# Ten row tiles of a Strassen-style projection are turned by VectorE blocks instead of TensorE transposes

## The chip, the cores and the metric

The kernel runs on one core of a Trainium2 chip. The core has TensorE (PE in the profile; its weight loads are the row PEld), VectorE (DVE), ScalarE (ACT), GpSimd (POOL) and SyncE (SP), which here only issues DMAs. The engines run side by side, each through its own queue in order. The metric is the device time of one execution in microseconds, as a median over runs.

## The reference

One graph attention layer over 2708 nodes of 1024 features, in float32, with a sparse 0/1 adjacency (about four neighbours a row):

```python
h = jnp.maximum(_layernorm(x, axis=-1), 0.0)
q = h @ W_q.T + b_q
k = h @ W_k.T + b_k
v = h @ W_v.T + b_v
z = scale * (q @ k.T)
spare_z = z * adj
spare_z = jnp.where(spare_z == 0.0, -10000.0, spare_z)
attn = jax.nn.softmax(spare_z, axis=1)
x = x + jax.nn.relu(attn @ v)
```

## The kernel before

**The mathematics.** W_q and W_k are folded into one matrix M, so that the score of an edge is the dot product of a row of `q = h M + b` with the neighbour's row of h. W_v is applied after the weighted sum: `u` is the sum of the neighbours' h rows by their softmax weights, and the output is `x + relu(u W_v + b)`. Nodes are sorted by their number of neighbours and cut into 21 full tiles of 128 rows; tile t has K[t] neighbour slots, from 1 to 15.

**Two products of tiles.** Both `h M` and `u W_v` are worked in pairs of row tiles (`units`: ten pairs of kind `q`, then ten of kind `o`, then one tile alone). A pair is a Strassen-style product with seven block products instead of eight (`multiply`, `opened`, `add_block`). Each of the seven is eight matmuls of 128x512 on PE as the chain shows them, four calls in the program, each in two passes. Its left operands are blocks of the turned (transposed) pair: `a11` and `a12`, the halves of the first tile, `a22`, a half of the second, and `s1 = a22 + a21`, `s3 = a11 - a21`, `s2 = s1 - a11`, `s4 = a12 - s2`. The right operands lie in `M` and `T` in SBUF. In a pair PE goes through `s2`, `a12`, `s4`, `s3`, then the first two products of the next pair (`a11`, `s1`), then `a22`.

**Where the operands come from.** `blocks` (L677) makes them one pair ahead, in two steps: `upper` (L692) at place 0 of the pair before, `lower` (L696) at place 2; the places are the calls of `after(i)` between the products. `half_turned` (L397) has PE transpose four 128x128 blocks into a PSUM bank; ScalarE copies the bank for `a11`, `a12` and `a22` (L684), VectorE adds and subtracts `a21` straight from PSUM for `s1` and `s3` and makes `s2` and `s4` (L688). Only in two early pairs are `s2` and `s4` on GpSimd.

**The stream.** Between those, VectorE works through the attention (`scores`, `weights`, `sums`): a multiply with a running sum for each neighbour slot (L826, output `junk`), small steps for the softmax, and a multiply-add for each slot (L879, into `u`). GpSimd gathers the neighbour rows by indirect DMA into 13 slots (`fill`, L805, and `gather`, L594); a slot is gathered anew as soon as it is read out. `advance(share)` at each place lets the stream go on by a quota of nominal microseconds, 19 for a pair of kind `o`. The order of VectorE's instructions is the program's (a manual schedule); ScalarE, GpSimd and SyncE are ordered by the framework's scheduler in this stretch.

**The tiles through DRAM.** The stream runs ahead of the `o` pairs. A finished `u` that is needed soon stays in SBUF (`near`, L933, `held`). Ten of the 21, tiles 6, 5, 4, 3, 2, 0, 1 and 20, 18, 19, are written to `u_dram` (L888) and read back into `or` tiles by one DMA each (L1142). The pairs are (6,5), (4,3), (2,0), (1,7), (13,12), (11,10), (14,9), (15,16), (20,17), (18,19), and tile 8 alone. Row tiles come from one ring of seven buffers (`row_tile`).

**The PSUM banks.** Each pair has banks X, Z and Y. Y starts as a copy of X that ScalarE makes (L961, `psy<-ps`) once `a11` is in X; the product with `s2` is added to this copy, so PE's first product of a pair needs it. ScalarE's queue also holds steps of the stream, which wait for VectorE.

## Time and profile before

| what | value |
|---|---|
| time of the runs | median 647.43 us (647.41 to 647.71, 3 runs) |
| profiled execution, its span | 641.9 us |
| TensorE busy | 635.2 us (99%) |
| VectorE busy | 521.9 us (81%) |
| GpSimd, ScalarE busy | 377.3 us (59%), 279.6 us (44%) |
| stretch of one `o` pair | 25.8 us |
| DMA | mean 294 GB/s |

The pairs of kind `o` start at about 372 us, and from 346 us on their operands are made. Each row of a timeline below gives the start in microseconds from the span's beginning, the duration, the engine, the line, the operation, the tiles out<-in with their shapes, and in brackets the idle time before it and what ended it. A row with x2 at its end is two instructions merged. In a row of waits the numbers are the total in microseconds, the number of waits and the longest.

### The profile page before, as it was taken

Reading aid. Unit: us, or ns where it says so; the run is one execution under the profiler, and the core shown is the slowest. Engines: PE = TensorE matmul, PEld = TensorE weight load, DVE = VectorE, ACT = ScalarE, POOL = GpSimd, SP = SyncE. Lnnn points to the kernel's source line nnn. Section 1 sums busy time; section 2 is a strip of 40 time slices with the busy share of each in tenths; the row PEclk is TensorE's granted clock in tenths of the full one; section 3 lists DMA queues with packets and bytes.
Section 4 is the critical chain, followed back from the end, with each engine's and each line's share of the span. In section 5 each row is a group of like instructions: output and inputs, shape, how many; then the busy total and the mean of one; then the engine's idle time right before and its main releaser. Section 6 shows DMA issues by size and latency. Waiting matters only on the chain.

```text
span 641.9 us, 6381 instructions
## 1 busy us (share of the span) xinstructions
PE 635.2 (99%) x1731; PEld 326.2 (51%) x1731; DVE 521.9 (81%) x1014; ACT 279.6 (44%) x426; POOL 377.3 (59%) x400
## 2 busy tenths in 40 slices
PE   9999999999999999999999999999999999999996
PEld 5777766444544444444444454454454444444442
DVE  5999788997895755998888959997999989989121
ACT  3539974849775622423223132433342344333300
POOL 2649960875858457755735525665685856872431
PEclk9999999999999999999999999999999999999999
DMA  8999997598798969998977998988898989995542
GB/s 338 407 366 314 345 346 295 189 358 301 264 358 317 363 201 404 355 359 257 322 260 275 419 416 267 327 272 255 240 328 272 283 331 304 281 285 125 146 139 95
DMA packets 61986, 189.02 MB, mean 294 GB/s; under 512 B 10701, under 2 KB 11037, under 8 KB 61048
## 3 DMA queue, kind: packets, MB, share of 16 engines
q0 software_dynamic: 27888, 84.95, 41.6%
q1 hardware_dynamic: 29994, 89.36, 37.7%
q10 hardware_dynamic: 4062, 14.24, 5.9%
q8 instruction: 16, 0.26, 0.2%
q14 instruction: 26, 0.21, 0.1%
HBM read 159.81 MB, written 42.31 MB: 315 GB/s over the span
## 4 chain that ended last, share of the span: by engine, by line
PE 98%; DMA 1%; DVE 0%; POOL 0%; POOLq 0%; issue 0%
PE ps L948 45%; PE psy L948 32%; PE ps_y L463 6%; PE pt L402 6%; PE ps_x L463 4%; PE ps_z L463 4%; DMA wlow<-in_wq_dram 1%; PE ps_h L1153 0%; PE ps_v L581 0%; DVE y_alone L1297 0%; POOL out_dram L1281 0%; POOLq L1303 0%; PE ps_all L664 0%; PE ps_in L662 0%; PE ps_b L728 0%
## 5 line engine op out<-in xcount | busy, mean ns | idle before, releaser
L597 POOL DMA_INDIRECT g<-h_dram,tab x105 | 124.8, 1188 | 70.4 <-ACT u L871 19.1
L948 PE MATMUL ps<-M,a 128*128 128x512 f32 x320 | 144.0, 593 | 0.0
L948 PE MATMUL psy<-wlow,s 128*128 128x512 f32 x320 | 143.9, 592 | 0.0
L826 DVE SCALAR_TENSOR_TENSOR junk<-g,pq 128x1024 uint8<-128x1024 f32 x93 | 114.0, 1226 | 9.8 <-DMA g<-h_dram,tab 7.3
L879 DVE SCALAR_TENSOR_TENSOR u<-g,coef,u 128x1024 f32<-128x1024 f32 x79 | 101.4, 1283 | 5.6 <-ACT u L871 3.7
L948 PEld LDWEIGHTS ps<-M,a 128*128 128x128 f32 x320 | 59.3, 190 | 68.0 <-issue 67.4
L948 PEld LDWEIGHTS psy<-wlow,s 128*128 128x128 f32 x320 | 59.2, 190 | 66.8 <-issue 65.8
L376 DVE FIND_INDEX8 at<-ones,adj 128x8 uint32<-128x685 f32 (+1 forms) x88 | 74.5, 865 | 0.0
L948 PE MATMUL psy<-wlow,a 128*128 128x512 f32 x160 | 71.9, 592 | 0.0
L948 PE MATMUL ps<-M,s 128*128 128x512 f32 x160 | 71.9, 592 | 0.0
L948 PE MATMUL ps<-wlow,s 128*128 128x512 f32 x160 | 71.9, 592 | 0.0
L355 ACT ACTIVATE sized<-adj 128x2708 uint8<-128x2708 f32 (+1 forms) x22 | 54.3, 2468 | 7.7 <-DMA adj<-in_adj_dram 6.4
L285 POOL TENSOR_TENSOR hsum<-hsum,x 128x256 f32<-128x256 f32 (+1 forms) x56 | 38.6, 726 | 26.3 <-DVE wlow L431 22.3
L1047 POOL DMA_INDIRECT y<-in_x_dram,tab x19 | 33.5, 1763 | 30.8 <-ACT taken L1013 11.2
L948 PEld LDWEIGHTS psy<-wlow,a 128*128 128x128 f32 x160 | 30.4, 190 | 38.3 <-issue 37.8
L948 PEld LDWEIGHTS ps<-wlow,s 128*128 128x128 f32 x160 | 30.4, 190 | 38.3 <-issue 37.6
L948 PEld LDWEIGHTS ps<-M,s 128*128 128x128 f32 x160 | 30.3, 190 | 38.1 <-issue 37.4
L778 POOL DMA_INDIRECT out_dram<-y,tab x21 | 28.4, 1353 | 19.3 <-DMA y<-in_x_dram,tab 11.6
L684 ACT COPY a<-pt 128x512 f32<-128x512 f32 x60 | 33.4, 590 | 3.1 <-PE pt L402 3.1
L597 POOL DMA_INDIRECT M<-h_dram,tab x20 | 24.2, 1212 | 13.4 <-ACT u L871 4.7
L688 DVE TENSOR_TENSOR s<-a,pt 128x512 f32<-128x512 f32 x40 | 25.6, 681 | 7.8 <-ACT a L684 7.8
L871 ACT ACTIVATE u<-g,coef 128x1024 f32<-128x1024 f32 x16 | 18.4, 1149 | 27.1 <-DVE coef L870 26.3
(238 smaller groups left out, 847.9 us busy)
## 6 DMA issues: line engine op xcount, KB each, us to landing
adj<-in_adj_dram SPq DMA_DIRECT2D x21, 1354.0 KB, 12.0
x<-in_x_dram SPq DMA_DIRECT2D x21, 512.0 KB, 8.0
h_dram<-x ACTq DMA_DIRECT2D x21, 512.0 KB, 7.2
q_late<-q SPq DMA_DIRECT2D x12, 512.0 KB, 6.9
pq<-q_late SPq DMA_DIRECT2D x12, 512.0 KB, 4.8
u_dram<-u SPq DMA_DIRECT2D x10, 512.0 KB, 6.5
or<-u_dram SPq DMA_DIRECT2D x10, 512.0 KB, 8.2
g<-in_wv_dram SPq DMA_DIRECT2D x16, 256.0 KB, 8.3
```

Of the source, the lines that this page charges most:

```text
L285: small.append(nc.gpsimd.tensor_add(hsum[:n, cols], hsum[:n, cols], xt[:n, cols]))
L355: nc.scalar.activation(sized[:n], a[:n, :, :PW], AF.Abs, accum_out=total[:n, t:t + 1])
L376: nc.vector.max_index(at[:n, k - first_k, g, :], ones[:n, 0:8], a[:n, g, :])
L402: nc.tensor.transpose(pt[:, c, :], xt[:, k * P:(k + 1) * P], ident)
L463: mm = nc.tensor.matmul(bank, a_tile(o + H * a[0], a[1], i), b(o), start=first and o == 0, stop=(o == H - 1), skip_group_check=True)
L597: return nc.gpsimd.indirect_dma_start(out=dst, out_offset=None, in_=src, in_offset=off, bounds_check=N - 1, oob_is_err=False)
L684: nc.scalar.copy(ops[name], bank)
L778: to = nc.gpsimd.indirect_dma_start(out=out, out_offset=bass.IndirectOffsetOnAxis(ap=ptab.bitcast(U32)[:n, t, SLOTS:SLOTS + 1], axis=0), i ...
L826: chained(lambda: nc.vector.scalar_tensor_tensor(junk, g_of[t][s], 1.0, tq[t], op0=ALU.mult, op1=ALU.mult, accum_out=zall[:, t, s:s + 1]))
L879: chained(lambda: nc.vector.scalar_tensor_tensor(u, g_of[t][s], coef[:, at[t][s]:at[t][s] + 1], u, op0=ALU.mult, op1=ALU.add))
L948: mm = nc.tensor.matmul(bank, a[:, c, :], b[:, c, :], start=False, stop=(c == 3), skip_group_check=True)
L1047: return nc.gpsimd.indirect_dma_start(out=y[:n], out_offset=None, in_=x, in_offset=off, compute_op=ALU.add)
```

## The change

The ten tiles that go through DRAM are no longer transposed by TensorE. VectorE can transpose 32-by-32 blocks inside each group of 32 partitions; what must move between the groups of partitions is moved by the DMA.

- When `u` of such a tile is done, ScalarE copies it once into a tile `v` in which the columns stand in quarter order (columns (c, a, r) at (a, c, r), with a one of four quarters and r one of 32), and `v` is written to `u_dram`.
- The tile is read back by four DMAs (`by_quarters`). Quarter a of the columns of all 128 rows lands on 32 partitions, in pieces of 256 elements (1 KB).
- `faces` is one VectorE instruction that transposes 128 partitions x 512 elements in 32-by-32 blocks and writes the half in its final order, straight into the operand tile in SBUF. `upper` makes `a11` and `a12` by it, `lower` `a22` and, in the tile of `s3`, `a21`; `s1` and `s3` are then made of SBUF operands.
- In a pair with such a tile (six pairs) `s2` and `s4` go to GpSimd.
- The stream's quota is cut by 0.75 nominal microseconds for each such tile of the next pair.

```diff
+QUADS = 4
+QP = P // QUADS
+FACED = (6, 5, 4, 3, 2, 0, 1, 20, 18, 19)
...
+    faced = []
+
+    def by_quarters(dst, rows):
+
+        faced.append(dst)
+        for a in range(QUADS):
+            cols = slice(a * D // QUADS, (a + 1) * D // QUADS)
+            nc.sync.dma_start(dst[a * QP:(a + 1) * QP, :].rearrange("r (g j) -> r g j", g=QUADS),
+                              rows[:, cols].rearrange("(g r) j -> r g j", r=QP))
+
+    def faces(dst, xt, lo, hi):
+
+        return nc.vector.transpose(dst.rearrange("p c (g r) -> p g c r", r=QP),
+                                   xt.rearrange("p (g c r) -> p g c r", g=QUADS, r=QP)[:, :, lo:hi])
+
+    def is_faced(xt):
+        return any(xt is y for y in faced)
+
...
+        def faced_half(name, xt, s):
+            ops[name] = small(name).rearrange("p (c q) -> p c q", q=P)
+            faces(ops[name], xt, s * 4, s * 4 + 4)
+
         def upper():
-            held("a11", half_turned(xa, 0))
-            held("a12", half_turned(xa, 1))
+            for s, name in enumerate(("a11", "a12")):
+                if is_faced(xa):
+                    faced_half(name, xa, s)
+                else:
+                    held(name, half_turned(xa, s))
 
         def lower():
-            held("a22", half_turned(xb, 1))
-            a21 = half_turned(xb, 0)
-            put("s1", ops["a22"], a21, ALU.add)
-            put("s3", ops["a11"], a21, ALU.subtract)
+            if is_faced(xb):
+                faced_half("a22", xb, 1)
+                faced_half("s3", xb, 0)
+                put("s1", ops["a22"], ops["s3"], ALU.add)
+                behind.append(nc.vector.tensor_sub(ops["s3"], ops["a11"], ops["s3"]))
+            else:
+                held("a22", half_turned(xb, 1))
+                a21 = half_turned(xb, 0)
+                put("s1", ops["a22"], a21, ALU.add)
+                put("s3", ops["a11"], a21, ALU.subtract)
             put("s2", ops["s1"], ops["a11"], ALU.subtract, eng)
             put("s4", ops["a12"], ops["s2"], ALU.subtract, eng)
...
-        if near(t):
+        if t in FACED:
+            v = row_tile(f"v_{t}")
+            nc.scalar.copy(v.rearrange("p (a c r) -> p c a r", a=QUADS, r=QP),
+                           u.rearrange("p (c a r) -> p c a r", a=QUADS, r=QP))
+            nc.sync.dma_start(u_dram[t * P:(t + 1) * P, :], v)
+        elif near(t):
             held[t] = u
...
-                nc.sync.dma_start(rows[-1], u_dram[t * P:(t + 1) * P, :])
+                if t in FACED:
+                    by_quarters(rows[-1], u_dram[t * P:(t + 1) * P, :])
+                else:
+                    nc.sync.dma_start(rows[-1], u_dram[t * P:(t + 1) * P, :])
...
         nxt = units[n + 1] if n + 1 < len(units) else None
+        if nxt is not None and nxt[0] == "o":
+            share -= 0.75 / 7 * len(set(nxt[1:]) & set(FACED))
...
-                    ops_of[n + 1] = blocks(*rows_of[n + 1], nc.gpsimd if n + 1 < FIRST - 1 else None)
+                    ops_of[n + 1] = blocks(*rows_of[n + 1], nc.gpsimd if n + 1 < FIRST - 1 or any(
+                        is_faced(xt) for xt in rows_of[n + 1]) else None)
```

How the instructions stand. On VectorE, the operands of the pair (6,5) amid the sums of tile 0, before (the sums s1 to s4 are all named s with a number, in the order s1, s3, s2, s4; `pt` is the bank that PE transposed into):

```order
L879 SCALAR_TENSOR_TENSOR u_2300<-g_1404,coef,u_2300 128x1024
L688 TENSOR_TENSOR s_2369<-a_2362,pt 128x512
L688 TENSOR_TENSOR s_2371<-a_2324,pt 128x512
L688 TENSOR_TENSOR s_2373<-s_2369,a_2324 128x512
L688 TENSOR_TENSOR s_2375<-a_2331,s_2373 128x512
L879 SCALAR_TENSOR_TENSOR u_2300<-g_1405,coef,u_2300 128x1024
```

and in the change (a_2335 and a_2337 are the halves of tile 6, a_2363 and s_2365 those of tile 5):

```order
L913 SCALAR_TENSOR_TENSOR u_2316<-g_1400,coef,u_2316 128x1024
L692 STREAM_TRANSPOSE a_2335<-or_2254 128x4x4x32
L692 STREAM_TRANSPOSE a_2337<-or_2254 128x4x4x32
L913 SCALAR_TENSOR_TENSOR u_2316<-g_1401,coef,u_2316 128x1024
L913 SCALAR_TENSOR_TENSOR u_2316<-g_1402,coef,u_2316 128x1024
L913 SCALAR_TENSOR_TENSOR u_2316<-g_1403,coef,u_2316 128x1024
L913 SCALAR_TENSOR_TENSOR u_2316<-g_1404,coef,u_2316 128x1024
L692 STREAM_TRANSPOSE a_2363<-or_2259 128x4x4x32
L692 STREAM_TRANSPOSE s_2365<-or_2259 128x4x4x32
L709 TENSOR_TENSOR s_2367<-a_2363,s_2365 128x512
L729 TENSOR_TENSOR s_2365<-a_2335,s_2365 128x512
L913 SCALAR_TENSOR_TENSOR u_2316<-g_1405,coef,u_2316 128x1024
```

Four block transposes have come in, and s2 and s4 have gone. They stand on GpSimd now, between two gathers of that pair's time:

```order
L600 DMA g_1403<-h_dram,tab 128x1024
L600 DMA g_1404<-h_dram,tab 128x1024
L709 TENSOR_TENSOR s_2370<-s_2367,a_2335 128x512
L709 TENSOR_TENSOR s_2372<-a_2337,s_2370 128x512
L600 DMA g_1405<-h_dram,tab 128x1024
```

where before the gathers stood behind each other. On ScalarE, around the copy `psy<-ps` that starts bank Y of the pair (14,9), before (w and m belong to tile 20 of the stream):

```order
L1013 COPY taken<-psy 128x512
L860 ACTIVATE w_3285,m_3324<-w_3285,m_3324 128x2
L865 ACTIVATE u_3326<-hsum,m_3324 128x1024
L1064 ACTIVATE y_3249<-u_3292 128x512
L961 COPY psy<-ps_3338 128x512
```

and in the change:

```order
L1052 COPY taken<-psy 128x512
L1103 ACTIVATE y_3217<-u_3259 128x512
L894 ACTIVATE w_3253,m_3304<-w_3253,m_3304 128x2
L1000 COPY psy<-ps_3292 128x512
L1003 COPY p_3359<-ps_3294 128x512
L899 ACTIVATE u_3306<-hsum,m_3304 128x1024
```

The 1024-element activation of tile 20 has moved behind the copy; the exponential, which waits for VectorE, still stands ahead of it. On VectorE, the operands of the last pair (18,19) amid the sums of tile 8, before:

```order
L879 SCALAR_TENSOR_TENSOR u_3675<-g_1400,coef,u_3675 128x1024
L688 TENSOR_TENSOR s_3776<-a_3769,pt 128x512
L688 TENSOR_TENSOR s_3778<-a_3745,pt 128x512
L688 TENSOR_TENSOR s_3780<-s_3776,a_3745 128x512
L688 TENSOR_TENSOR s_3782<-a_3752,s_3780 128x512
L879 SCALAR_TENSOR_TENSOR u_3675<-g_1401,coef,u_3675 128x1024
```

and in the change:

```order
L913 SCALAR_TENSOR_TENSOR u_3642<-g_1399,coef,u_3642 128x1024
L692 STREAM_TRANSPOSE a_3726<-or_3672 128x4x4x32
L692 STREAM_TRANSPOSE s_3728<-or_3672 128x4x4x32
L709 TENSOR_TENSOR s_3730<-a_3726,s_3728 128x512
L729 TENSOR_TENSOR s_3728<-a_3712,s_3728 128x512
L913 SCALAR_TENSOR_TENSOR u_3642<-g_1400,coef,u_3642 128x1024
L913 SCALAR_TENSOR_TENSOR u_3642<-g_1401,coef,u_3642 128x1024
```

One multiply-add of tile 8 more stands behind the pair's s1.

## The prediction

> **What bounds the kernel now.** I read the page's engine shares and its chain of waits first, then the chain in order of time, then VectorE (DVE), GpSimd (POOL) and ScalarE (ACT) in the timeline around the ten tiles.
>
> ```profile
> span 641.9 us, 6381 instructions
> PE 635.2 (99%) x1731; PEld 326.2 (51%) x1731; DVE 521.9 (81%) x1014; ACT 279.6 (44%) x426; POOL 377.3 (59%) x400
> PE 98%; DMA 1%; DVE 0%; POOL 0%; POOLq 0%; issue 0%
> ```
>
> TensorE (PE) is the chain: 98% of the span. The profiled execution's span is 641.9 us, the median of the runs 647.43, so 5.5 us lie around the span; I make the sum on the span and add the difference to 647.43. Where DVE and POOL stand while the `o` pairs are worked, one pair's stretch to a row:
>
> ```profile
> core 0: us, PE busy (x) PEld busy (x) DVE busy (x) ACT busy (x) POOL busy (x), PEclk, DMA share, GB/s
> 346.86:372.65 25.79, 25.79 (x75) 12.30 (x73) 23.67 (x27) 5.46 (x10) 14.90 (x13) 1.00 1.02 411
> 475.79:501.57 25.78, 25.78 (x74) 12.29 (x73) 25.25 (x41) 9.14 (x17) 16.89 (x15) 1.00 0.91 302
> 578.93:604.71 25.78, 25.78 (x74) 12.29 (x73) 16.75 (x29) 7.32 (x13) 8.19 (x6) 1.00 0.51 132
> ```
>
> PE never pauses, but DVE is busy 23.67 and 25.25 of 25.79 us: it is the next bound, nearly level with PE until about 553 us. That decides this change, which takes from PE and gives to DVE.
>
> **What is removed.** The eight TensorE transposes of a tile:
>
> ```profile
> L402 PE MATMUL pt<-ident,or x80: 272/273/273, 346.7 to 583.8; 128*128 128x128 f32 x80
> 346.86 0.87 PE pt L402 x8
> 527.36 0.87 PE pt L402 x8
> 528.23 3.44 PE psy L948 x8
> 594.41 6.87 PE ps L948 x16
> ```
>
> The 273 ns are pipelined; on the chain eight cost 0.87 us. Ten tiles are 8.7 us: seven tiles (6.1 us) are turned from 346 us on, before the product at 528.23, and three (2.6 us) after it, up to 584. Full effect would be a span of 633.2.
>
> **What is added to DVE.** Twenty 32-by-32 block transposes of 128x512 and, moved off it, two subtractions (s2, s4) in each of six pairs.
>
> ```profile
> 352.44 1.28 DVE L688 TENSOR_TENSOR s<-a,pt 128x512 f32<-128x512 f32 x2
> 353.63 0.68 DVE L688 TENSOR_TENSOR s<-s,a 128x512 f32<-128x512 f32 x1
> 354.35 0.69 DVE L688 TENSOR_TENSOR s<-a,s 128x512 f32<-128x512 f32 x1
> 354.96 2.60 DVE L879 SCALAR_TENSOR_TENSOR u<-g,coef,u 128x1024 f32<-128x1024 f32 x2
> ```
>
> Start to start an operation of 512 elements takes 0.60 (352.44 to 353.63 for two), s2 and s4 together 1.33, one of 1024 elements 1.30. No block transpose stands in this trace: 0.60 is its lower bound, 1.25 (two passes over 512, the 1024-element rows) its upper. I take 0.65, near the rows of equal element count. s1 and s3 keep their 0.60.
>
> The page "VectorE: DVE Perf Modes" of the Trainium skill, section "The three transpose paths", gives 311 ns for 128x128 in bf16 on VectorE; four of those would be an estimate of 1.24 us, and with it the sum is that of the rival on dear transposes below. No run here shows it yet.
>
> **What the moved subtractions cost.** POOL did s2 and s4 of an early pair before, and VectorE's rows beside them are these; below each other POOL, DVE beside it, and the same DVE operations alone:
>
> ```profile
> 132.78 1.26 POOL L688 TENSOR_TENSOR s<-s,a 128x512 f32<-128x512 f32 x1
> 132.93 1.26 DVE L389 TENSOR_TENSOR cand<-first,at 128x128 f32<-128x128 f32 x1
> 134.12 1.27 POOL L688 TENSOR_TENSOR s<-a,s 128x512 f32<-128x512 f32 x1
> 134.22 1.31 DVE L390 SCALAR_TENSOR_TENSOR cand<-at,cand 128x128 f32<-128x128 uint32 x1
> 103.87 0.29 DVE L389 TENSOR_TENSOR cand<-first,at 128x128 f32<-128x128 f32 x1
> 32.60 3.84 POOL L543 TENSOR_TENSOR wq<-wq,wlow 128x512 f32<-128x512 f32 x2 [3.45 <-DMA adj<-in_adj_dram]
> 33.02 5.83 DVE L519 SCALAR_TENSOR_TENSOR acc_b<-wk,bq_sb,acc_b 128x1024 f32<-128x1024 f32 x3
> ```
>
> A 0.29 us operation of two SBUF operands took 1.26: it ended 0.15 us after POOL's. At 33.02 three operations that need 3.7 (three at 1.2, and an end) took 5.83, 2.1 more for two on POOL, 1.07 each. So a subtraction on POOL stops DVE for 1.07 to 1.27; I take 1.17, 2.34 a pair. What stands behind it on DVE is the stream's multiply-adds, all of two SBUF operands. A pair therefore costs DVE 1.0 more than the 1.33 it saves.
>
> The Trainium skill's page "SBUF — State Buffer", section "SBUF: two separate sides", calls that port pair an exclusive lock, held for a whole instruction; the rows above agree. By that rule moving s2 and s4 relieves nothing.
>
> **What DVE gets back.** It stops waiting where it is late itself:
>
> ```profile
> DVE junk L826 <- DMA g<-h_dram,tab: 7.3, 5, 2.1
> DVE s L688 <- ACT a L684: 3.4, 2, 2.2
> DVE u L1063 <- PE ps L948: 1.7, 1, 1.7
> 371.92 1.23 DVE L826 SCALAR_TENSOR_TENSOR junk<-g,pq 128x1024 uint8<-128x1024 f32 x1 [1.39 <-DMA g<-h_dram,tab]
> 375.20 1.23 DVE L826 SCALAR_TENSOR_TENSOR junk<-g,pq 128x1024 uint8<-128x1024 f32 x1 [2.05 <-DMA g<-h_dram,tab]
> 379.56 1.22 DVE L826 SCALAR_TENSOR_TENSOR junk<-g,pq 128x1024 uint8<-128x1024 f32 x1 [1.86 <-DMA g<-h_dram,tab]
> ```
>
> 5.1 us of waits for ScalarE and PE vanish, and 5.3 for gathers at 371.92 to 379.56, where the first eight new transposes come to lie: 10.4.
>
> **Two places where DVE holds PE.** First, PE's product that starts at 528.23 needs the copy of its bank on ACT, which stands behind an ACT step that waits for DVE's tile 20:
>
> ```profile
> 523.51 0.15 DVE L859 TENSOR_REDUCE m<-w 128x1 f32<-128x2 f32 x1
> 523.70 0.30 ACT L860 ACTIVATE w<-w,m 128x2 f32<-128x2 f32 x1 [6.02 <-DVE m L859]
> 523.90 0.19 ACT L860 ACTIVATION_READ_ACCUMULATOR w<-w,m 128x1 f32 x1
> 526.47 0.57 ACT L961 COPY psy<-ps 128x512 f32<-128x512 f32 x1
> 587.61 1.28 DVE L688 TENSOR_TENSOR s<-a,pt 128x512 f32<-128x512 f32 x2
> ```
>
> The copy ends 527.04, 1.2 before PE. In the changed order it follows that step directly, so DVE must end the reduce by 528.2 - 6.1 (PE earlier) - 1.1 (0.30, a 0.19 read of the sum and 0.57) = 521.0. DVE ends it at 523.66 (523.51 and 0.15), plus 0.60 for an addition now ahead of it, plus 14 x 0.65 = 9.1, plus 4 pairs x 1.0, minus 10.4: 527.0. PE stands 6.0 there: of 6.1 saved 0.1 is left, and the last three tiles add 2.6, so 2.7. Second, the last pair's s1, which PE needs at 594.41 + 3.43 = 597.85 (two products): it ends at 588.29 (the first of the two at 587.61, 0.68 long); plus 20 x 0.65 = 13.0, plus 5 x 1.0, minus 10.4, minus 1.31 for a multiply-add now behind it: 594.6, so PE is 3.2 earlier there. The later of the two binds: **2.7 us saved**, span 639.2, 644.7 by the median.
>
> **What costs nothing here.** Ten copies in quarter order on ACT, bound by the 1024-element activations and, at nothing, by what they replace: sixteen copies of 0.59 go. ACT is busy 5 to 9 us of 25.8; if it stood in the chain of a tile, 1.15 each. The reload:
>
> ```profile
> 342.13 1.15 ACT L871 ACTIVATE u<-g,coef 128x1024 f32<-128x1024 f32 x1 [0.73 <-DVE coef L870]
> or<-u_dram SPq DMA_DIRECT2D x10, 512.0 KB, 8.2
> q1 hardware_dynamic: 29994, 89.36, 37.7%
> 378.15 0.94 SPq L1142 DMA_DIRECT2D or<-u_dram x2
> ```
>
> SP issues 40 loads for 10: thirty more at 0.3 to 0.5 spread over 250 us. Pieces of 1 KB instead of rows of 4 KB: if a piece took as long as a packet of this queue (0.377 x 16 x 641.9 / 29994 = 0.13 us), a tile would take 512 x 0.13 / 16 = 4.1 us of the engines against 1.0; if time follows bytes, no more. The loads at 378.15 are used from 398 on, 20 us later against 8.2 to land, so lateness itself is covered; what 0 to 3.1 us a tile takes from the gathers is not, and I take nothing for it but keep it as a rival. Behind DVE's wait for a reload stand its evictions, which PE needs within 6 to 14 us. The smaller quota of the stream (0.75 a tile) moves steps later and removes none.
>
> **Rivals.** (a) DVE keeps room: POOL's subtractions fall into DVE's pauses or beside one-operand steps and lock nothing. Then the first place has 523.66 + 0.60 + 9.1 - 4 x 1.33 - 10.4 = 517.6, before 521.0; PE stays the bound and the whole 8.7 comes: **638.7**. For it: the waits quoted above are such pauses. Against: s1 stands last of the transposes, and two-operand steps follow.
> (b) Slower: a block transpose takes 1.25. The second place then gets 20 x 0.60 = 12.0 more, 597.85 - 3.2 + 12.0, and the end comes 8.8 later than before: **656.2**. It decides from 0.81 on (3.2 / 20 above 0.65). For it: the element is 4 bytes wide and the patterns are broken into runs of 32; against: equal element counts took equal time in every other DVE row.
> (c) Slower by DMA: a share of 1.02 stands at 346 to 372, and 1 KB pieces delay the gathers, so the 5.3 of gather waits don't vanish: 2.7 - 5.3, **650.0**.
> (d) Nothing to tell: the places above give back 8 to 9 of the 8.7, **647.4**.
>
> **Numbers.** DVE holds part of the gain: 0.43; (a) 0.17; (b) 0.17; (c) 0.15; (d) 0.08. The likeliest alone ranges over 642 to 648 (transposes 0.60 to 0.70 are 1 us either way, a locked subtraction 1.07 to 1.27 about 1). For 8 in 10 the range takes in (a) and (c) and leaves (b) and some edge out: 638.5 to 652.5. A change of 0.2% (1.3 us) is about what can be told from none. Faster: all of (a), 0.34 of the likeliest: 0.51; same: 0.07 of the likeliest and most of (d): 0.14; slower: (b), (c) and the rest: 0.35.
>
> **What would show it.** PE's transposes drop by 80 and its busy time by 8.7, with new pauses of some 6 us about 500 to 530 us, released by ACT copies behind DVE; block transposes of 0.65 to 0.75 us in their own row; multiply-adds on DVE of 2.4 us beside L688-like rows on POOL; gather waits near 375 gone. Wrong would be: no PE pauses (a), transposes above 0.81 (b), or VectorE's waits for gathers grown (c).

## The result, and the profile after

The change is slower by a hair: 649.16 us median (646.57 to 651.84, 14 runs) against 647.67 us (646.70 to 649.47, 14 runs), a ratio of 1.0015 with a 95% interval of 1.0001 to 1.0029. Eighty PE transposes are gone and the time is 1.5 us longer.

The first view is the page of the changed kernel: its span, engine shares and chain of waits by engine and by line.

```profile
span 647.9 us, 6298 instructions
PE 633.0 (98%) x1651; PEld 319.2 (49%) x1651; DVE 536.8 (83%) x1022; ACT 281.8 (43%) x420; POOL 396.3 (61%) x412
PE 88%; DVE 5%; DMA 2%; ACT 2%; issue 2%; another core or an unknown queue 1%; POOL 0%; POOLq 0%; ACTq 0%; SPq 0%; DVEq 0%
PE ps L987 39%; PE psy L987 29%; PE ps_y L466 6%; PE ps_x L466 4%; PE ps_z L466 4%; PE pt L405 4%; DMA wlow<-tv_dram 2%; DVE u L913 2%; DVE junk L860 1%; ACT sized L358 1%; PE ps_y L501 1%; ACT x L266 0%; DVE s L709 0%; PE ps_h L1195 0%
```

PE was 98% of the chain and is 88%: a load of weights (`wlow<-tv_dram`) and VectorE's sums stand in it now. The next view is PE's waits: engine, tile and line, what it waited for, microseconds in all, number of waits, the longest.

```profile
PE psy L987 <- DMA wlow<-tv_dram: 5.1, 1, 5.1
PE psy L987 <- ACT psy L1000: 1.9, 1, 1.9
PE ps_y L501 <- POOL hsum L115: 1.2, 1, 1.2
PE ps L987 <- DMA M<-in_wv_dram: 0.8, 1, 0.8
PE ps L987 <- DVE s L709: 0.6, 1, 0.6
```

The two waits for weights, `wlow` (a 1 MB block of the right operand T) and `M`, lie in the first `o` pair. PE's timeline there shows them in brackets:

```profile
374.86 3.60 PE L987 MATMUL psy<-wlow,s 128*128 128x512 f32 x8
379.29 3.70 PE L987 MATMUL ps<-M,a 128*128 128x512 f32 x8 [0.83 <-DMA M<-in_wv_dram]
383.09 3.67 PE L987 MATMUL ps<-M,s 128*128 128x512 f32 x8
391.85 6.49 PE L987 MATMUL psy<-wlow,s 128*128 128x512 f32 x8 [5.09 <-DMA wlow<-tv_dram]
408.47 1.88 PE L987 MATMUL psy<-wlow,s 128*128 128x512 f32 x4
```

In the kernel before, PE took the block of T that it waits for here (391.85) without a pause:

```profile
384.54 3.60 PE L948 MATMUL psy<-wlow,s 128*128 128x512 f32 x8
```

In the changed kernel, from the `s2` product of one pair (374.86) to that of the next (408.47) PE takes 33.6 us. Seven products at 3.43 start to start are 24.0, so 9.6 us are lost in this one pair: 5.1 and 0.8 of waiting, a product that took 6.49 instead of 3.60 because the granted clock fell after the pause (0.91 from 385 to 392 us, 0.65 from 392 to 400), and small rests. That is more than the 8.7 that the ten tiles save. The stretch before and after (start and end, then busy time of PE, PEld, DVE, ACT and POOL, granted clock, DMA share, GB/s), first of before:

```profile
372.00:400.00 28.00, 28.00 (x84) 13.69 (x83) 21.04 (x38) 8.65 (x17) 10.46 (x9) 1.00 0.95 332
```

and of after:

```profile
372.00:400.00 28.00, 21.98 (x45) 8.98 (x44) 21.94 (x34) 6.96 (x12) 10.93 (x9) 0.88 1.04 363
```

PE is idle for 6.0 of 28 us, its mean granted clock is down to 0.88, and DMA is full. What SyncE issued around it (start, duration of the issue, line, operation, tiles; x7 is seven merged, from the start of the first to the end of the last, with the queue's own pauses):

```profile
352.01 4.71 SPq L687 DMA_DIRECT2D or<-u_dram  x7
367.20 0.34 SPq L1061 DMA_DIRECT2D q_late<-q  x1
367.63 0.86 SPq L1292 DMA_DIRECT2D M<-in_wv_dram  x2
375.19 0.33 SPq L923 DMA_DIRECT2D u_dram<-v  x1
376.16 0.33 SPq L1061 DMA_DIRECT2D q_late<-q  x1
376.58 0.90 SPq L1292 DMA_DIRECT2D wlow<-tv_dram  x2
384.32 14.99 SPq L687 DMA_DIRECT2D or<-u_dram  x8
```

and before:

```profile
355.51 3.77 SPq L1247 DMA_DIRECT2D M<-in_wv_dram  x2
362.38 0.33 SPq L1247 DMA_DIRECT2D wlow<-tv_dram  x1
365.62 0.32 SPq L888 DMA_DIRECT2D u_dram<-u  x1
372.68 0.32 SPq L1247 DMA_DIRECT2D wlow<-tv_dram  x1
373.30 0.32 SPq L1022 DMA_DIRECT2D q_late<-q  x1
```

The last two blocks of T stand behind the last `q_late` store and go out at 376.58; before they went out at 362.38 and 372.68, one on each side of the store of `u_0` and both ahead of the last `q_late` store. All of this stretch lies 4.1 us later in this execution (next fence), so the first of the two is 10 us late and the second on time; the M loads, at 367.63 instead of 355.51, are 8 late. The first block landed 15.1 us after its issue, at 391.7. Eight reload DMAs, the quarters of two tiles, had been issued ahead of all of them, from 344 to 357.

One number serves all comparisons below. PE starts a product `ps_h` at the end of the `q` pairs; all that the change touches on PE lies behind it. First before, then after:

```profile
324.38 1.88 PE L1153 MATMUL ps_h<-hsum,ones 128*128 128x512 f32 x4
328.51 1.88 PE L1195 MATMUL ps_h<-hsum,ones 128*128 128x512 f32 x4
```

From this start to the end of the span is the **tail**: 641.9 - 324.4 = 317.5 before, 647.9 - 328.5 = 319.4 after. The tail grew by 1.8: 9.6 lost in the first pair and 0.6 in the wait for `s`, less 8.7 saved, make 1.5 of it. The 4 us that the two spans differ ahead of it are not the change's, as the first experiment shows.

### The profile page after: what moved, and what is told of

It reads as the page before. It is cut to its first block, busy times and chain, and to the rows that moved or that the text cites. A ratio compares the mean times of both kernels' runs of the same rounds, so it can differ in the third digit from the quotient of the medians.

```text
span 647.9 us, 6298 instructions
## 1 busy us (share of the span) xinstructions
PE 633.0 (98%) x1651; PEld 319.2 (49%) x1651; DVE 536.8 (83%) x1022; ACT 281.8 (43%) x420; POOL 396.3 (61%) x412
## 3 DMA queue, kind: packets, MB, share of 16 engines
q1 hardware_dynamic: 34314, 89.36, 38.7%
## 4 chain that ended last, share of the span: by engine, by line
PE 88%; DVE 5%; DMA 2%; ACT 2%; issue 2%; another core or an unknown queue 1%; POOL 0%; POOLq 0%; ACTq 0%; SPq 0%; DVEq 0%
PE ps L987 39%; PE psy L987 29%; PE ps_y L466 6%; PE ps_x L466 4%; PE ps_z L466 4%; PE pt L405 4%; DMA wlow<-tv_dram 2%; DVE u L913 2%; DVE junk L860 1%; ACT sized L358 1%; PE ps_y L501 1%; ACT x L266 0%; DVE s L709 0%; PE ps_h L1195 0%
## 5 line engine op out<-in xcount | busy, mean ns | idle before, releaser
L600 POOL DMA_INDIRECT g<-h_dram,tab x105 | 127.3, 1212 | 55.3 <-issue 21.0
L987 PE MATMUL psy<-wlow,s 128*128 128x512 f32 x320 | 148.6, 608 | 7.0 <-DMA wlow<-tv_dram 5.1
L860 DVE SCALAR_TENSOR_TENSOR junk<-g,pq 128x1024 uint8<-128x1024 f32 x93 | 116.0, 1247 | 2.6 <-DMA pq<-q_dram,tab 0.8
L913 DVE SCALAR_TENSOR_TENSOR u<-g,coef,u 128x1024 f32<-128x1024 f32 x79 | 106.1, 1343 | 5.2 <-ACT u L905 3.1
L987 PEld LDWEIGHTS psy<-wlow,s 128*128 128x128 f32 x320 | 61.1, 195 | 80.0 <-issue 70.7
L1086 POOL DMA_INDIRECT y<-in_x_dram,tab x19 | 30.6, 1609 | 14.9 <-issue 4.3
L600 POOL DMA_INDIRECT M<-h_dram,tab x20 | 22.5, 1125 | 12.8 <-issue 4.9
L616 POOL DMA_INDIRECT tab_dram<-tab,pos_i x22 | 22.4, 1020 | 11.1 <-DVE pos_i L676 5.6
L709 DVE TENSOR_TENSOR s<-a,pt 128x512 f32<-128x512 f32 x32 | 20.5, 681 | 9.8 <-ACT a L705 5.7
```

The costliest lines, as they stand in the source:

```text
L600: return nc.gpsimd.indirect_dma_start(out=dst, out_offset=None, in_=src, in_offset=off, bounds_check=N - 1, oob_is_err=False)
L616: put = nc.gpsimd.indirect_dma_start(out=tab_dram[lo >= EARLY][:, :], out_offset=bass.IndirectOffsetOnAxis(ap=pos_i[:n, t:t + 1], axis=0), ...
L860: chained(lambda: nc.vector.scalar_tensor_tensor(junk, g_of[t][s], 1.0, tq[t], op0=ALU.mult, op1=ALU.mult, accum_out=zall[:, t, s:s + 1]))
L913: chained(lambda: nc.vector.scalar_tensor_tensor(u, g_of[t][s], coef[:, at[t][s]:at[t][s] + 1], u, op0=ALU.mult, op1=ALU.add))
L987: mm = nc.tensor.matmul(bank, a[:, c, :], b[:, c, :], start=False, stop=(c == 3), skip_group_check=True)
L1086: return nc.gpsimd.indirect_dma_start(out=y[:n], out_offset=None, in_=x, in_offset=off, compute_op=ALU.add)
```

## The experiments

All ratios are to the kernel before on the same chip, with 95% intervals. The tail is of the profiled execution. "Waits" are PE's behind `ps_h`. The whole-row reload and the four reloads of 32 whole rows leave out the exchange between the groups of partitions, so their ten tiles do not hold the reference's values; only their times are used.

| run | ratio | tail, us | PE's waits in the tail, us |
|---|---|---|---|
| before, again | (one run) | 317.7 | none |
| the change | 1.0015 (1.0001 to 1.0029) | 319.4 | wlow 5.1, M 0.8, s 0.6 |
| last three tiles alone | 0.997 (0.9958 to 0.9982) | 315.2 | none |
| early seven alone | 1.0046 (1.0030 to 1.0063) | 320.8 | wlow 5.1, M 0.9, issue 0.7 |
| loads earlier | 0.9958 (0.9937 to 0.9980) | 315.3 | DVE 2.6 and 1.2, M 0.9 |
| s2, s4 on VectorE | 1.0048 (1.0033 to 1.0064) | 320.4 | wlow 3.3, M 2.0, s 0.6 |
| whole-row reload | 0.9916 (0.9903 to 0.9928) | 312.5 | DVE 2.0 and 1.2 |
| loads earlier, s on VectorE | 0.9954 (0.9936 to 0.9972) | 315.9 | DVE 1.9 and 1.2, M 1.6, ACT 1.3 |
| before, late order | 1.0006 (0.9997 to 1.0015) | 318.3 | s 0.5 |
| four reloads of 32 whole rows | 0.9985 (0.9969 to 1.0001) | 316.9 | wlow 3.8, issue 0.6 |
| quarters at the store | 0.9938 (0.9920 to 0.9955) | 313.8 | DVE 2.9 |
| quarters at the store, s on VectorE | 0.9895 (0.9870 to 0.9920) | 310.7 | DVE 1.2 |
| before, 1 KB pieces | 1.0001 (0.9988 to 1.0014) | 317.7 | none |
| before, 32 partitions | 1.0041 (1.0028 to 1.0055) | 319.0 | or 1.2 |
| before, 32 partitions, late order | 1.0046 (1.0023 to 1.0070) | 319.6 | or 1.3, s 0.2 |
| before, 1 KB pieces, late order | 1.0005 (0.9992 to 1.0017) | 317.7 | none |
| quarters at the store, late order | 0.9973 (0.9959 to 0.9988) | 313.9 | wlow 3.9, s 0.6 |

### The kernel before, again

> The kernel before, unchanged, for a second profile of it. In the changed kernel's profile ScalarE waits 2.5 and 2.7 us between 168 and 192 us for something that the profile cannot name, and PE's first product there starts at 192.43 us instead of 186.86; the instructions of that stretch are the same in both kernels. Theory: that stall belongs to most executions of either kernel, and the shown profile of before (span 641.9, 5.5 us under its median) was one without it. Then this profile has a span of about 646 us and PE stands some 4 us in 165 to 193 us. Rival: the stall is the change's own. Then this profile has again about 642 us of span and no such wait.

One run, 647.88 us, span 646.2. ScalarE's timeline of it:

```profile
171.53 0.59 ACT L992 COPY u<-psy 128x512 f32<-128x512 f32 x1 [2.34 <-remote]
178.88 0.59 ACT L1026 COPY q<-ps 128x512 f32<-128x512 f32 x1 [1.40 <-remote]
```

The stall is there without the change, and the tail of 317.7 is that of the first profile within 0.2. The shown profile of before was an execution without it (its `ps_h` starts at 324.38, here at 328.48). Tails can be compared; spans can't.

### Which tiles: the last three, and the early seven

```diff
-FACED = (6, 5, 4, 3, 2, 0, 1, 20, 18, 19)
+FACED = (20, 18, 19)
```

> Only tiles 20, 18 and 19 are faced; the seven early tiles are as before. Twenty-four PE transposes go, 2.6 us by 0.87 for eight. Theory (the gain of the early seven is lost because the weight loads of the first o pair come late): nothing is lost here, 647.7 - 2.6 = 645.1, ratio 0.996. Rival (a transpose taken from PE is worth less than 0.87 for eight, because PE's stream has slack somewhere else): within 0.5 us of before, ratio 0.999 to 1.000. Rival (VectorE's added time holds PE in the last pairs): 647 or more.

Ratio 0.997, tail 2.4 shorter than the 317.6 of before (the mean of its two profiles), and the medians 2.1 apart: saved transposes are worth close to the 2.6 that the chain said for three tiles.

```diff
-FACED = (6, 5, 4, 3, 2, 0, 1, 20, 18, 19)
+FACED = (6, 5, 4, 3, 2, 0, 1)
```

> Only tiles 6, 5, 4, 3, 2, 0 and 1 are faced. Fifty-six PE transposes go, 6.1 us. Theory: the whole loss lies with these seven, since the late weight loads (5.1 and 0.8 us of PE waits and a product of 6.49 us instead of 3.60) and PE's short waits at 498 to 528 us come with them: 1.5 + 2.6 above before, 651.8, ratio 1.006, and the wait for wlow of about 5 us near 386 us stands in this profile too. Rival: the loss is shared with the last three tiles; then the time is at or under before's 647.7.

Ratio 1.0046, tail 3.2 longer, with the same wait of 5.1 for `wlow`. The whole loss lies with the early seven: 6.1 saved and 9.3 paid.

### The loads written earlier

```diff
-            for k, at in enumerate(((0, 0), (0, 1), (0, 3), (0, 4), (0, 5), (0, 6), (1, 2))):
+            for k, at in enumerate(((0, 0), (0, 1), (0, 3), (0, 3), (0, 4), (0, 5), (0, 6))):
```

> The changed kernel with the loads of the o product's weights written one place earlier in the program, so that in SyncE's queue the loads of M's parts and of the next block of T stand ahead of the late q store and of the store of v_0, and only the last block behind them. Nothing else moves. Theory (late loads): PE's wait of 5.1 us for wlow near 386 us and the slow product behind it go, wholly or for the larger part; 5 to 8 us less than the changed kernel's 649.2, so 641 to 644, ratio 0.990 to 0.995. Rival (VectorE's time is what bounds the stretch 372 to 528 us, so that whatever PE gains early it gives back at 498 to 528): PE's waits move there, 647 to 649. Rival (the DMA engines, not the queue's order, are late: share 1.02 to 1.08 there): the loads land no earlier, 648 to 650.

Ratio 0.9958, tail 315.3: 4.1 of the changed kernel's 319.4 come back, short of the 5 to 8 us that the theory asked. The wait for `wlow` is gone. In its place stand waits for VectorE:

```profile
509.80 1.06 PE L405 MATMUL pt<-ident,u 128*128 128x128 f32 x8 [2.62 <-DVE u L913]
525.77 3.67 PE L987 MATMUL ps<-wlow,s 128*128 128x512 f32 x8 [1.17 <-DVE s L709]
```

So both held: late weights were the first bound, and VectorE stood close behind. The changed kernel had shown only 0.6 of the second, as one would expect where PE has lost the time before.

### s2 and s4 on VectorE

```diff
-                    ops_of[n + 1] = blocks(*rows_of[n + 1], nc.gpsimd if n + 1 < FIRST - 1 or any(
-                        is_faced(xt) for xt in rows_of[n + 1]) else None)
+                    ops_of[n + 1] = blocks(*rows_of[n + 1], nc.gpsimd if n + 1 < FIRST - 1 else None)
```

> The changed kernel with s2 and s4 of the six pairs on VectorE again, so that nothing on GpSimd locks it; SyncE's order is that of the changed kernel, the last two blocks of T still stand behind the last q store. Theory (the order in SyncE's queue makes the weights late): the q store of tile 18 no longer waits about 7 us for VectorE, so the wait of 0.8 us for M and the 0.6 us for s near 528 us go, but the 5.1 us for wlow and the slow product stay: 647.5 to 648.5. Rival (the lock on VectorE makes the weights late, by way of the late q store): PE's wait for wlow goes too, 641 to 643.

Slower than expected, 1.0048, and the waits stay: 3.25 for `wlow` and 1.96 for `M`, with both products behind them slow.

```profile
376.51 5.40 PE L987 MATMUL ps<-M,a 128*128 128x512 f32 x8 [1.96 <-DMA M<-in_wv_dram]
388.59 6.68 PE L987 MATMUL psy<-wlow,s 128*128 128x512 f32 x8 [3.25 <-DMA wlow<-tv_dram]
```

The lock of GpSimd on VectorE is not what makes the weights late. The `q_late` store came earlier, but only by 1.5 us: 361.53 is 37.2 after this execution's `ps_h` (324.37), 367.20 in the changed kernel is 38.7 after.

### The reload as one DMA of whole rows

```diff
-                    by_quarters(rows[-1], u_dram[t * P:(t + 1) * P, :])
+                    faced.append(rows[-1])
+                    nc.sync.dma_start(rows[-1], u_dram[t * P:(t + 1) * P, :])
```

> The changed kernel with each faced tile read back by one DMA of whole 4 KB rows instead of four of 1 KB pieces. The blocks then lie on the wrong partitions, so this kernel's output for the ten tiles is not the reference's; every engine has the same instructions as in the changed kernel, and SyncE has 30 DMAs fewer. With them SyncE's order changes: the last two blocks of T stand ahead of the last q store again. Theory (the order): no wait for wlow, and the time of the kernel with the loads written earlier, 645 to 646. Rival (the 1 KB pieces also take the DMA engines' time): 1 to 3 us less than that kernel, 642 to 644.

Ratio 0.9916, tail 312.5, the size that the rival for the pieces had: 5.1 of 8.7 arrive. PE waits for no weights, only for VectorE:

```profile
501.95 1.06 PE L405 MATMUL pt<-ident,u 128*128 128x128 f32 x8 [1.98 <-DVE u L913]
517.91 3.67 PE L987 MATMUL ps<-wlow,s 128*128 128x512 f32 x8 [1.16 <-DVE s L709]
```

But four things changed at once: the pieces, the number of issues, the partitions that one DMA lands on, and SyncE's order. The next runs part them.

### Loads earlier and s on VectorE together

The edits of "loads earlier" and "s2 and s4 on VectorE".

> Loads written earlier (as in the kernel that measured 645.1) and s2 and s4 of the six pairs on VectorE. In that kernel PE still waits 2.6 us at 509.8 for VectorE's multiply-adds and 1.2 us at 525.8 for s. Theory (a subtraction on GpSimd costs VectorE 1.17 and saves it 0.67, so that a pair on GpSimd loses 1.0): five pairs give VectorE 5 us before 526, both waits go and PE takes the whole saving: 641 to 642. Rival (GpSimd's share relieves VectorE): 6 x 1.33 us come on top, PE waits longer, 646 or more.

Neither theory: 0.9954, as without the second edit. VectorE's busy time fell by 3.7 us (537.1 to 533.4 on the pages), but at 401.90 it then waited 3.9 us for a reload by quarters:

```profile
401.90 1.30 DVE L692 STREAM_TRANSPOSE a<-or 128x512 f32<-128x512 f32 x2 [3.93 <-DMA or<-u_dram]
```

### The late order alone, in the kernel before

```diff
-                    nc.sync.dma_start(place, src)
+                    with tc.issue_after(stored[-1].ins) if k > 4 else nullcontext():
+                        nc.sync.dma_start(place, src)
```

(`stored` holds the `q` stores.)

> The kernel before, with nothing faced, but the loads of the last two blocks of T set behind the last q store in SyncE's queue, the order of the changed kernel. They are issued at about 373.8 us instead of 362.4 and 372.7. Theory (the queue's order alone costs): with the 15.1 us from issue to landing of the changed kernel the block lands at 389, and PE, which needs it at 384.5, stands up to 4.5 us and then runs slow: 650 to 655. Rival (late only because the reloads by quarters fill the DMA engines): it lands within 8 to 10 us, by 384, and the time is before's, 647.5 to 648.5.

The theory missed: no wait for weights, 1.0006. Issued at 374.46, the block was there when PE wanted it at 385.29, 10.8 us later. In this kernel the order alone costs nothing.

### Four reloads of 32 whole rows

```diff
-            cols = slice(a * D // QUADS, (a + 1) * D // QUADS)
-            nc.sync.dma_start(dst[a * QP:(a + 1) * QP, :].rearrange("r (g j) -> r g j", g=QUADS),
-                              rows[:, cols].rearrange("(g r) j -> r g j", r=QP))
+            nc.sync.dma_start(dst[a * QP:(a + 1) * QP, :], rows[a * QP:(a + 1) * QP, :])
```

> The changed kernel with four reload DMAs a tile as there, but each of 32 whole rows of 4 KB. The blocks then lie on the wrong partitions, so the output for the ten tiles is not the reference's. Every queue has the changed kernel's instructions in the changed kernel's order; only the pieces grow from 1 KB to 4 KB. Theory (the 1 KB pieces keep the DMA engines busy twice as long for their bytes, so that weights queued behind them land late): PE's wait for wlow falls from 5.1 us to 1 or less, and the ratio to before is near that of the single whole-row DMA, 0.992 to 0.994. Rival (four times the issues, and the queue's order that they bring, make the weights late): the wait stays at 3 to 5 us, ratio 1.000 or more.

The wait for `wlow` stays at 3.75 us with 4 KB rows, so the 1 KB pieces are not the whole cause:

```profile
379.10 0.94 SPq L1290 DMA_DIRECT2D wlow<-tv_dram  x2
391.39 6.29 PE L985 MATMUL psy<-wlow,s 128*128 128x512 f32 x8 [3.75 <-DMA wlow<-tv_dram]
```

They seem to have a share, though. The wait for `M` is gone, PE has the block 12.3 us after its issue instead of 15.3 (376.58 to 391.85), and the ratio is 0.9985 instead of 1.0015. What the whole-row reload lacks and this one has is four issues, each onto 32 partitions, and the late order.

### 1 KB pieces or 32 partitions, in the kernel before

Four runs with the TensorE transposes untouched. First four reloads of a quarter of the columns each:

```diff
-                nc.sync.dma_start(rows[-1], u_dram[t * P:(t + 1) * P, :])
+                for a in range(4):
+                    cols = slice(a * D // 4, (a + 1) * D // 4)
+                    nc.sync.dma_start(rows[-1][:, cols], u_dram[t * P:(t + 1) * P, cols])
```

> The kernel before, nothing faced, TensorE transposes as they were; only the ten reloads are made by four DMAs of a quarter of the columns each, 128 pieces of 1 KB, to the places where they belong. This is the suspected cost by itself. Theory (pieces): with the 1.3 us of all DMA engines that a tile's pieces take above whole rows, PE waits for M or wlow some 1 to 4 us, though the loads of T stand ahead of the last q store here; ratio 1.002 to 1.008. Rival (the pieces cost only because the changed kernel's queue also has the loads behind a late store): 0.999 to 1.001.

Then four reloads of 32 rows each:

```diff
+                for a in range(4):
+                    part = slice(a * 32, (a + 1) * 32)
+                    nc.sync.dma_start(rows[-1][part, :], u_dram[t * P:(t + 1) * P, :][part, :])
```

> The kernel before, nothing faced; each of the ten reloads by four DMAs, each of 32 whole rows of 4 KB onto 32 partitions. Bytes, issues and places are those of the kernel with quarter columns onto 128 partitions, which kept 390 to 430 GB/s and cost nothing. Theory (a DMA that lands on 32 partitions alone slows the DMA engines): the rate falls to 270 to 330 GB/s for some 12 us around 352 to 368 us; the last two blocks of T still stand around the late q store, so PE waits 0 to 2 us: ratio 1.000 to 1.003. Rival (the number of issues was what slowed it): the rate stays over 390.

Each of them with the late order:

> As the kernel before with reloads of 32 rows onto 32 partitions, and the loads of the last two blocks of T behind the last q store, the order of the changed kernel. Each alone: the order cost nothing. Theory (both are needed: slow DMA and weights queued behind the late store): PE waits 2 to 5 us for wlow near 388 us and runs slow behind it; ratio 1.004 to 1.010. Rival (VectorE's lock, which made the q store 7 us later, was needed as well): no wait, 0.999 to 1.001.

> The same late order with the four reloads a tile of a quarter of the columns each: 1 KB pieces, 128 partitions. Theory (32 partitions, not the pieces and not the issues): the rate stays over 390 GB/s, the wait for wlow is under 1 us, ratio 0.999 to 1.002. Rival (pieces or issues slow the weights): as with 32 partitions, 1.004 or more.

What the DMA engines moved from 340 to 400 us, in 40 slices of 1.5 us, first with 32 rows a DMA (above it the share of time that the engines were busy, in tenths; 9 is 90% or more):

```profile
DMA  7006999999999999999999999999999999999999
GB/s 292 0 0 137 366 322 341 423 399 399 421 270 281 262 268 265 311 423 393 429 432 412 415 421 426 383 445 412 407 432 412 429 399 330 232 251 279 257 257 232
```

then with a quarter of the columns a DMA (the run with the late order),

```profile
GB/s 303 46 0 60 246 395 340 445 383 241 299 418 408 409 404 410 392 412 416 421 404 418 418 412 396 418 412 423 423 434 434 412 418 406 368 342 370 244 219 312
```

the changed kernel,

```profile
GB/s 281 68 0 109 350 368 298 415 396 328 328 293 311 319 341 323 325 339 322 355 404 402 413 426 421 421 402 407 421 421 431 437 410 423 407 330 161 212 173 193
```

and the kernel before as first shown:

```profile
GB/s 60 257 410 412 431 415 355 300 426 407 426 431 421 426 423 423 410 426 399 429 429 421 394 407 437 421 402 415 421 415 412 366 328 279 74 298 107 186 240 311
```

In the slices right behind the eighth reload issue (12 to 16, 356.5 to 364 us; the eighth is out at 356.3 to 356.7 in the first three), four issues a tile of 1 KB pieces onto 128 partitions leave the core's whole traffic at 404 to 418 GB/s (the two slices of 241 and 299 ahead of them have a like in the kernel before, 355 and 300, three slices earlier as its stretch is). Four issues of the same bytes in 4 KB rows onto 32 partitions push it down to 262 to 281, and the changed kernel stands at 293 to 341 for ten slices. So landing on 32 partitions is what is slow, while the engines count as full, and it slows what is in flight with it: with the late order in both, the queue of the gathers moved 7.41 MB in this window with 32 partitions and 8.32 MB with 128. By itself that costs the kernel before 0.41%, some 2.5 us between the medians; the profiled tail is 1.4 longer, of which 1.2 is PE's wait for a reload at 558 us. Onto 128 partitions, pieces and number of issues cost nothing (1.0001).

The expectation for 32 partitions with the late order missed: PE did not wait for `wlow` there either.

```profile
378.62 0.92 SPq L1252 DMA_DIRECT2D wlow<-tv_dram  x2
389.44 3.60 PE L948 MATMUL psy<-wlow,s 128*128 128x512 f32 x8
```

That kernel still transposes on PE, which reaches the block at 60 us after `ps_h`, some three later than the changed kernel does (391.85 less the two waits of 5.09 and 0.83 is 57.4 after its own, and 56.8 in the changed kernel with four reloads of 32 whole rows). The later arrival does not explain it alone: the block was there at most 10.8 us after its issue, where the changed kernel's took 15.1. The low rate lasted six slices there and ten in the changed kernel; whether that is the reason was not tested.

### The quarters exchanged at the store

```diff
-            nc.sync.dma_start(u_dram[t * P:(t + 1) * P, :], v)
+            for g in range(QUADS):
+                cols = slice(g * D // QUADS, (g + 1) * D // QUADS)
+                nc.sync.dma_start(u_dram[t * P:(t + 1) * P, cols].rearrange("(a r) j -> r a j", r=QP),
+                                  v[g * QP:(g + 1) * QP, :].rearrange("r (a j) -> r a j", a=QUADS))
...
-                              rows[:, cols].rearrange("(g r) j -> r g j", r=QP))
+        nc.sync.dma_start(dst, rows)
```

> The changed kernel with the exchange of quarters moved from the reload to the store: v goes to u_dram by four DMAs of 1 KB pieces, in the order in which a plain DMA of whole 4 KB rows reads it back. The bytes and the pieces are as many, but five of the seven early stores lie between 260 and 325 us. Theory (pieces cost where DMA is full and weights wait behind them): the waits for M and wlow go, and PE keeps what VectorE leaves it, the ratio of the whole-row reload: 0.991 to 0.994. Rival (the pieces cost the gathers of the earlier stretch as much): 0.996 to 1.000.

Ratio 0.9938, no wait for weights. Five of the seven early stores lie ahead of the crowded stretch, the first of the last two blocks of T goes out ahead of the last `q_late` store again, and the reload is one DMA onto 128 partitions. Only VectorE holds PE:

```profile
507.83 1.48 PE L405 MATMUL pt<-ident,u 128*128 128x128 f32 x8 [2.89 <-DVE u L910]
```

With s2 and s4 on VectorE as well:

> The quarters exchanged at the store, and s2 and s4 of the six pairs on VectorE. With the loads written earlier, this second edit saved VectorE 3.7 us of busy time, but it then waited 3.9 us for a reload. Theory (the reload was what hid it): without late reloads PE's waits for VectorE of about 2 us and 1.2 us near 500 to 520 us shrink by 2 us or more, ratio 0.987 to 0.990. Rival (those two waits hang on a gather or on PE's own results, not on VectorE's time): as with GpSimd, within 0.1% of the other kernel.

Ratio 0.9895 (641.12 us against 648.19): **the version that beats both**, with 6.9 of the 8.7 us in the tail. PE's one wait left:

```profile
520.36 3.67 PE L987 MATMUL ps<-wlow,s 128*128 128x512 f32 x8 [1.17 <-DVE s L706]
```

With the reload out of the way the lock does matter: VectorE's busy time falls from 536.0 to 532.8, and 3.7 us of time go with it.

And with the late order put back (the edit shown above, in the first of these two kernels):

> The kernel with the quarters exchanged at the store (ratio 0.994), with the loads of the last two blocks of T set behind the last q store, as the changed kernel has them. Its reloads are whole rows onto 128 partitions. Theory (in the changed kernel the slow reloads and the late order add up, since PE comes 3.5 us earlier to these weights than the kernel before does; in the kernel before the same order left the weights just in time): about 10.5 us from issue to landing instead of 15, so PE waits 1 to 3 us for wlow; ratio 0.995 to 0.999. Rival (the late order does nothing without the slow reloads): no wait, ratio as without it, 0.992 to 0.9955. Rival (the order is the whole cause): a wait of 4 us or more, 0.999 to 1.002.

```profile
389.78 3.67 PE L987 MATMUL psy<-wlow,s 128*128 128x512 f32 x8 [3.89 <-DMA wlow<-tv_dram]
```

PE waits 3.9 us, more than expected, and the median says 0.9973: between the theory and the order as sole cause. So the late order and PE's earlier arrival are enough for a wait, without slow reloads. In this profile the block is there 11.4 us after its issue instead of 15.1, and no slow product comes behind the wait; the loads of `M`, which the edit leaves alone, go out early here (358.45), and PE does not wait for them. The profiled tail (313.9) is the same as without the order (313.8), since the wait of 2.9 us for VectorE is gone: a wait here takes the place of one later. The runs' ratios put the order at 2.3 us (0.9973 against 0.9938), this one profile at nothing. The profiled execution was the fastest of the twelve (644.66 against a median of 647.38), so it may not stand for the others; the difference stays open.

## Why the prediction was wrong

It said 644.7 us (638.5 to 652.5) and faster as likeliest; 649.16 lies inside the range, on the other side of before. By its own steps:

- **What is removed: right.** 8.7 us on the chain; the last three tiles alone gave 2.4 of 2.6 in the tail.
- **The block transposes: right.** 0.65 was taken, 0.60 to 1.25 were the bounds. The changed kernel's instructions of that line (count, then shortest, median and longest in ns, first and last start):

```profile
L692 DVE STREAM_TRANSPOSE a<-or x16: 667/704/707, 352.9 to 597.9; 128x512 f32<-128x512 f32 x16
```

  The two that start at 352.92 are followed by the next instruction at 354.14, 0.61 each. The rival with 1.25 fell.
- **The lock: the mechanism right, the size close, its place in the sum small.** Beside s2 and s4 on GpSimd, VectorE's rows:

```profile
362.05 4.49 DVE L913 SCALAR_TENSOR_TENSOR u<-g,coef,u 128x1024 f32<-128x1024 f32 x2
386.61 2.29 DVE L860 SCALAR_TENSOR_TENSOR junk<-g,pq 128x1024 uint8<-128x1024 f32 x1
388.82 1.21 DVE L902 SCALAR_TENSOR_TENSOR w<-w,keys 128x7 f32<-128x7 f32 x1
```

  The first pair of rows takes 4.49 instead of the 2.60 of two; the others 2.29 for 1.22 and 1.21 for 0.16. That is 1.9 and 2.1 a pair of tiles, where 2.34 was taken. In the two kernels with the quarters at the store it is 3.7 us of time; with slow reloads it did not show. With the loads earlier the two kernels are level (0.9958 and 0.9954), and the changed kernel without the lock was slower (1.0048 against 1.0015), with two slow products behind its waits instead of one.
- **The first place where VectorE holds PE: half right.** PE was to stand 6.0 us at the copy `psy<-ps`. That copy held PE in none of the tails. With weights on time (the whole-row reload) PE stands 2.0 and 1.2 us at 502 and 518, for the sums of a tile that stays in SBUF and for `s1`: 3.1 in all. The second place, the last pair's `s1`, held nothing.
- **The step that failed is "What costs nothing here", the reload.** It asked whether the reloaded tiles would be late for their own use, found 20 us of room, and took nothing. It named the gathers as what could suffer, not the 1 MB blocks of T and M that stand in the same queue, behind a store that waits for the end of the `q` pair. It costed the pieces of 1 KB, which cost nothing onto 128 partitions, and not the 32 partitions, which do. And it left out that SyncE's order could move: here the last two blocks of T fell behind the last `q_late` store, while in the kernel before thirty more reload DMAs alone left the first of them ahead (370.66 against 377.26 with 32 rows a DMA). The changed kernel's profile puts about 9.6 us at the term that was taken as nothing: PE arrives 3 us earlier at weights that arrive later. Rival (c) named the right engine, and that its time (650.0) is near is luck: it was 2.7 us of gain less 5.3 of gather waits that stay, and the gather waits near 375 did vanish.

The Trainium skill has the rule that was passed over: its page "SBUF — State Buffer", section "Door 1: The DMA port swizzle (why `[64,N]` ≈ `[32,N]`)", says that a DMA's rate goes by how many of 16 ports its partitions reach, that 32 partitions reach 8, and gives 189 against 328 GB/s for 1 MB. The runs agree in direction: all traffic fell to 262 to 281 from 404 to 418 while such reloads were in flight.

Settled by the runs: where the time went (weights of the first `o` pair), that reloads onto 32 partitions slow the DMA engines, that pieces and issues do not when they land on 128, and that with the exchange at the store and s2 and s4 on VectorE 6.9 of the 8.7 us arrive. Either mend alone takes back more than the loss: the loads earlier (0.9958), or the reload onto 128 partitions with the two blocks of T still late in the queue (0.9973). How the 9.6 us divide between the slow reloads, the late order and PE's earlier arrival stays open; with fast reloads the order alone is between 0 and 2.3 us.

## What to carry to other kernels

Time taken from the bound engine brings it earlier to every transfer that doesn't move, so ask at the next weights, not only at the edited tiles, what is due and what stands ahead of it in its queue. A reshaping DMA should touch all 128 partitions on the side where the traffic is dense; here the same exchange, moved from the reload to the store, turned 0.15% slower into 0.6% faster, with most of those stores outside the dense stretch. And a wait that is taken away may uncover another just behind it: gains and losses of single waits don't add up, so run the combination.

## What the runs showed of the hardware that was not expected

- Onto 32 partitions, 4 KB rows took the rate further down (262 to 281 GB/s) but for five slices of 1.5 us, 1 KB pieces less far (293 to 341) but for ten. These are two different kernels; in the changed kernel itself the block of T came sooner with 4 KB rows (12.3 against 15.3 us after its issue).
- Eight reload issues spread over 15.0 us of SyncE's queue at 384.32 in the changed kernel, and over 13.5 us with 128 partitions; two plain ones took 0.9. The issues are short (a median of 0.43 us in the changed kernel). By its profile the queue stood 8.1 us until loads of `wlow` had landed and 3.8 us for two other transfers. In neither case did PE wait for what stood behind them.
- After a pause of 5.09 us a product took 6.49 us instead of 3.60, after 3.25 us 6.68, after 1.96 us 5.40, but after 3.89 us only 3.67, with the granted clock at 1.00 throughout. The length of the pause alone doesn't say when the granted clock falls.
- An execution may hold a stall of some 4 us between 168 and 193 us that has nothing to do with the kernel's edits. The first profile of before was free of it, which is why its span lay 5.5 us under the median of the runs, while 1.7 us is the usual distance between an execution's time and its span (649.56 and 647.9 for the changed kernel). It may go with the chip: the four profiles from the chip on which the kernel before ran 644.04 us were free of it too, with `ps_h` at 324.4 to 325.1 us; in all the others it starts at 328.3 or later, and there the kernel before ran 647.7 to 648.9 us.
